# A fused binary-convolution and attention kernel: weight chunks for two blocks at once, packing one block behind the signs, and the last image's tiles moved to other memory

## The chip, the cores and the metric

The kernel runs on one core of one Trainium2 chip. The metric is the time of one execution in device microseconds (us). A ratio is the mean time of one kernel's undisturbed runs over the mean time of the kernel before in the same rounds on the same chip, with a 95% interval; it is therefore not exactly the ratio of the medians that are quoted beside it.

## The reference

Sixteen images of 256 channels and 28 x 28 pixels go through four layers. The two layers with sign weights, and the normalization between them, are where the change works:

```python
def layer0(x, weights, gamma, beta):              # first layer
    out = sign(x)                                  # forward value of the straight-through form
    scaling = mean(abs(weights), axis=(1, 2, 3))   # one number per output channel
    y = conv3x3(out, sign(weights)) * scaling      # (summed in slices of 64, saturating)
    yn = batchnorm(y) * gamma + beta
    return yn + x
# second layer: residual = prelu(x); clipped 3x3 convolution, fixed normalization, prelu, gate 1,
#               residual; then a 1x1 convolution, normalization, prelu, gate 2, residual.
#               gate = sigmoid(relu(mean(mix) @ w1 + b1) @ w2 + b2)
# third layer:  batchnorm -> sign -> conv3x3(sf * sign(w1)) -> prelu -> batchnorm -> sign
#               -> conv3x3(sf * sign(w2)) -> prelu -> batchnorm -> + x -> prelu
# fourth layer: attention over the pixels with 64 channels, projection, + x
```

## The kernel before

A 3x3 convolution of an image half ("block", 392 pixels) with sign weights is done in two ways. For five of six weight chunks the signs of two groups of 128 output channels are packed into one number, so 15 matmuls do the work of 30; the sixth chunk is done plainly with six matmuls, and two more unpack. `packed` is followed by a rounding on ScalarE and VectorE.

```python
def sign(k, g):                                     # one weight chunk of 384 KB, already loaded in st
    ...
    sg = tmp.tile([P, 3, 256], BF16, tag="sg", bufs=1)
    A.activation(sg, st, AF.Sign)                   # ScalarE
    V.scalar_tensor_tensor(dst[0][:, n], sg[:, :, P:], PACK, sg[:, :, 0:P], mult, add)   # VectorE: wpk
def add_up(k, g):                                   # sums of |w| for the scaling
    V.tensor_reduce(ab, st..., add, apply_absolute_value=True)                           # VectorE: ab
    return lambda: total_up(k, g, ab)               # TensorE "sumabs<-ones,ab", then VectorE "sf"
def both(first, second):                            # a step: sign + pack + reduce; its sum one block later
    return [Step(f.load, lambda: (f.work(), s.work())[1]) ...]

def packed(j):                                      # 15 matmuls of block j
    for n in range(5):
        for t in range(3): product(j, ..., w[0][:, n, t, :], ...)
    A.activation(r, pss[j], Identity, bias=rounding, scale=1/PACK); V.tensor_scalar(bs[j], r, -ROUND, None, add)

# sign_layer, for each block j:  packed(j); plain(j-1); post(j-1); signs of the next image;
#                                late();  late = steps.pop(0)()
```

The start loads the small parameters `vec`, the first image whole, and each weight chunk, which is signed and packed at once with the single `sg` buffer. At the end of the second layer two squeeze gates are computed, each by four small matmuls `hid` and four small matmuls `gate`. TensorE is given filler matmuls (`keep_busy(n)`, all on a tile `idle`) in front of and behind them, so that its clock stays up:

```python
keep_busy(14); g = gates(hidden_b(B, hidden_a(B)));  keep_busy(14)     # gate 1 of the last image
... conv1x1(b) ...
unit_u(b, 0); unit_u(b, 1, True)                    # u of the last image, tiles of tag "yu" in pool ph1
keep_busy(14); h = hidden_a(B + 1); ... g = gates(h)[:, 1] ...; keep_busy(14)          # gate 2
sg1, bg1 = norm("l2a", moments1, ...);  branch2(b, k, g) for both k    # gate updates that read u
# ph1 is released here; the third layer's padded image buffer "fpads" lies in the released memory
fpads = float_pads(ph, "fpads")                     # four clearings of its rim, on GpSimd
keep_busy(12)
```

## Time and profile before

| | us |
|---|---|
| median of 3 runs | 1153.67 (1153.47 to 1154.21) |
| span of the profiled run | 1151.9, mean granted clock 0.991 |
| TensorE busy | 1113.7 (97%) |
| first 30 packed matmuls loaded, by the weight loads | 19.74 |
| first gate ("hid") at the end of the second layer | 524.66 |
| second gate to the third layer's first convolution matmul | 539.10 to 547.30 = 8.20 |
| those first 30 matmuls | 7.65 |

The lines behind these numbers stand in the prediction below. In a timeline a row is start, duration, engine, kernel line, operation, output<-inputs, count, and in brackets the idle time before it with what ended it. A row with "x26" is 26 instructions run together. The rows "PE ... unused<-idle" are the fillers: the work is thrown away, but their spacing shows the clock, about 0.22 us at full clock ("warm" below) and 0.43 at half ("cold").

### The profile page before, as it was taken

The page shows a single profiled execution, that of the slowest core. Times are in us where ns is not written, and L with a number is a line of the kernel's source. Part 1 is how long each engine was busy: PE and PEld are TensorE (multiplying, and loading weights), DVE is VectorE, ACT ScalarE, POOL GpSimd, SP SyncE. Part 2 cuts the span into 40 slices and gives each one's busy share as a digit, 9 for nine tenths or more (in the row PEclk, how much of TensorE's full clock was granted, in tenths as well). Part 3 has the DMA queues.
Part 4 walks back from the last instruction along what each step waited for, and adds up shares of the span by engine and source line. Part 5 has one row for each costly group of instructions (what it writes and reads, how often), then busy time and mean ns, then how long its engine had stood idle before and what let it go on. Part 6 is the DMA issues. An engine that isn't in the chain of part 4 may idle for free.

```text
span 1151.9 us, 15800 instructions
## 1 busy us (share of the span) xinstructions
PE 1113.7 (97%) x6062; PEld 948.5 (82%) x6067; DVE 801.2 (70%) x1430; ACT 711.5 (62%) x1051; POOL 135.8 (12%) x134
## 2 busy tenths in 40 slices
PE   6998999999999999998999999999999999999995
PEld 6998989999999999994999998999955555555542
DVE  3775359899999999967576665566574667666565
ACT  4654445677777777765555554555576766767742
POOL 2000000000000000000000000000013443443421
PEclk9999999999999999999999999999999999999998
DMA  7553341222222231010680000000014355464422
GB/s 301 187 178 140 126 143 40 71 98 85 91 106 84 74 124 70 29 53 34 249 317 5 1 1 1 1 1 1 1 57 112 95 158 147 106 168 122 131 84 87
DMA packets 25973, 111.63 MB, mean 97 GB/s; under 512 B 3554, under 2 KB 6308, under 8 KB 25892
## 3 DMA queue, kind: packets, MB, share of 16 engines
q1 hardware_dynamic: 20436, 80.85, 20.0%
q0 software_dynamic: 5456, 29.71, 8.8%
q8 instruction: 50, 0.82, 0.3%
q14 instruction: 31, 0.25, 0.1%
HBM read 65.59 MB, written 44.96 MB: 96 GB/s over the span
## 4 chain that ended last, share of the span: by engine, by line
PE 79%; issue 5%; DVE 4%; ACT 2%; POOL 0%; POOLq 0%; ACTq 0%; DVEq 0%
PE cv L248 24%; PE cv L574 23%; PE sc L1127 7%; PE av L1148 7%; PE mi L1112 4%; PE sm L1188 4%; PE cv L678 3%; PE cv L267 2%; PE mi L1198 2%; PE unused L342 1%; PE sm L1148 1%; ACT fpads L933 1%; DVE r L1173 0%; PE hid L506 0%; PE gate L649 0%
## 5 line engine op out<-in xcount | busy, mean ns | idle before, releaser
L248 PE MATMUL cv<-fpads,wpk 128*128 128x392 f32 x1440 | 297.9, 360 | 11.3 <-DVE wpk L208 8.9
L574 PE MATMUL cv<-vs,w 128*128 128x392 f32 x1536 | 301.4, 354 | 0.0
L574 PEld LDWEIGHTS cv<-vs,w 128*128 128x128 f32 x1536 | 287.4, 190 | 1.6 <-issue 0.3
L248 PEld LDWEIGHTS cv<-fpads,wpk 128*128 128x128 f32 x1440 | 274.8, 194 | 15.7 <-issue 8.5
L963 DVE SCALAR_TENSOR_TENSOR p<-r,r,cv 128x392 f32<-128x392 f32 x128 | 78.6, 614 | 79.5 <-ACT r L960 79.5
L1131 ACT ACTIVATE es<-sc 112x784 f32<-112x784 f32 x112 | 87.2, 822 | 73.8 <-PE sc L1127 73.6
L248 PE MATMUL cv<-fpads,wpl 128*128 128x392 f32 x576 | 124.8, 352 | 0.0
L259 ACT ACTIVATE t<-cv,rounding 128x392 f32<-128x392 f32 x96 | 56.2, 586 | 88.0 <-PE cv L248 85.7
L248 PEld LDWEIGHTS cv<-fpads,wpl 128*128 128x128 f32 x576 | 108.9, 190 | 0.6
L1127 PE MATMUL sc<-q,k 64*112 64x392 f32 x448 | 89.0, 510 | 2.6 <-DVE k L1119 1.6
L960 ACT ACTIVATE r<-cv 128x784 f32<-128x784 f32 (+1 forms) x66 | 52.9, 805 | 60.0 <-PE cv L267 59.5
L260 DVE TENSOR_SCALAR uv<-t 128x392 fp32r<-128x392 f32 x96 | 35.0, 364 | 68.1 <-ACT t L259 68.1
L1148 PE MATMUL av<-es,va 112*64 112x392 f32 x448 | 80.8, 499 | 0.0
L1127 PEld LDWEIGHTS sc<-q,k 64*112 64x112 f32 x448 | 35.8, 172 | 43.3 <-issue 18.3
L1141 POOL TENSOR_TENSOR sum<-sum,es 112x784 f32<-112x784 f32 x32 | 68.5, 2139 | 2.5
L1148 PEld LDWEIGHTS av<-es,va 112*64 112x64 f32 x448 | 29.6, 136 | 47.4 <-issue 44.6
L103 DVE TENSOR_TENSOR vs<-pad 128x840 fp32r<-128x840 bf16 (+1 forms) x66 | 64.5, 1002 | 0.1
L481 ACT CAST n<-cv 128x784 int16<-128x784 f32 x32 | 26.0, 812 | 58.8 <-DVE l_parts L480 16.4
L1119 DVE COPY k<-mi 64x784 f32<-64x784 f32 x16 | 15.6, 976 | 64.2 <-ACT q L1118 64.2
L716 POOL DMA_DIRECT2D x2d<-x x16 | 8.5, 533 | 366.8 <-DVE x L710 304.0
L1202 DVE TENSOR_TENSOR p<-mi,p 128x784 f32<-128x784 f32 x30 | 29.2, 975 | 31.5 <-PE mi L1198 31.1
L1188 PEld LDWEIGHTS sm<-wv,p 128*112 128x112 f32 x448 | 46.7, 178 | 5.0 <-issue 2.6
(248 smaller groups left out, 1702.7 us busy)
## 6 DMA issues: line engine op xcount, KB each, us to landing
xs<-in_x_dram SPq DMA_DIRECT2D x32, 784.0 KB, 4.4
x2d<-x POOLq DMA_DIRECT2D x16, 784.0 KB, 3.6
xd<-p SPq DMA_DIRECT2D x16, 784.0 KB, 3.3
out_dram<-p SPq DMA_DIRECT2D x15, 784.0 KB, 5.3
p<-x2d SPq DMA_DIRECT2D x13, 784.0 KB, 9.0
p<-x2d POOLq DMA_DIRECT2D x13, 784.0 KB, 9.1
n0d<-n POOLq DMA_DIRECT2D x16, 392.0 KB, 2.7
n<-n0d SPq DMA_DIRECT2D x16, 392.0 KB, 3.1
```

The lines of the kernel that those rows point to most:

```text
L103: V.tensor_tensor(o, a, b, op)
L248: T.matmul(pss[j][:, mo, :HN].rearrange("p (a b) -> p a b", b=S), lhsT=lhsT, rhs=pads[:, j // 2 % 2, k, r:r + HR, c:c + S], start=start, s ...
L259: A.activation(r, pss[j][:, 0, :HN], AF.Identity, bias=rounding, scale=1.0 / PACK)
L574: T.matmul(ps.rearrange("p (a b) -> p a b", b=S), lhsT=w[:, k, c, u, mo * P:(mo + 1) * P], rhs=vs[:, b % 2, u, k, :, c:c + S], start=(n == 0),
L960: A.activation(r[:, mo], ps[:, mo, :HN], AF.Relu, scale=-1.0)
L963: V.scalar_tensor_tensor(p, r[:, mo], beta[:, mo:mo + 1], ps[:, mo, :HN], ALU.mult, ALU.add)
L1112: T.matmul(ps[:, h, :HN], lhsT=wqk[:, k, :], rhs=x[b][:, k, h * HN:(h + 1) * HN], start=(k == 0), stop=(k == 1),)
L1127: T.matmul(ps[:MC, h, :HN], lhsT=k_[rows, c * MC:(c + 1) * MC], rhs=qs[b][rows], start=True, stop=True)
L1131: A.activation(e, ps[:MC, :, :HN], AF.Exp, scale=0.125)
L1141: (V if late else nc.gpsimd).tensor_tensor(sums[b, late], sums[b, late], e, ALU.add)
L1148: T.matmul(ps[64 * h:64 * h + 64, :HN], lhsT=w, rhs=e[:, h, :], start=start, stop=stop)
L1188: T.matmul(ps[:MC, c * 64:(c + 1) * 64], lhsT=x[b][:, k, c * MC:(c + 1) * MC], rhs=wv[:, k, :], start=(k == 0), stop=(k == 1),)
```

## The change

Three things are intended: TensorE starts sooner, because two blocks use each weight chunk as it comes and the transfers are in the order of need; VectorE reduces before it packs, so the weight sums no longer wait; and the third layer's buffer can be cleared early, because the last image's `u` no longer lies in the memory that it takes. The core of the diff:

```diff
-    nc.sync.dma_start(out=vec, in_=d["vecs"])
+    nc.gpsimd.dma_start(out=vec, in_=d["vecs"])
@@ sign: returns the packing instead of doing it; two sg buffers at the start
-            sg = tmp.tile([P, 3, 256], BF16, tag="sg", name="sg", bufs=1)
-            A.activation(sg, st, AF.Sign, saturate=False)
-            V.scalar_tensor_tensor(dst[0][:, n], sg[:, :, P:], PACK, sg[:, :, 0:P], ALU.mult, ALU.add)
+            t = tmp.tile([P, 3, 256], BF16, tag=sg[0], name="sg", bufs=sg[1])
+            A.activation(t, st, AF.Sign, saturate=False)
+            return lambda: V.scalar_tensor_tensor(
+                dst[0][:, n], t[:, :, P:], PACK, t[:, :, 0:P], ALU.mult, ALU.add
+            )
@@ both: packing and sum run one block later
-        return [Step(f.load, lambda f=f, s=s: (f.work(), s.work())[1]) for f, s in zip(first, second)]
+        def work(f, s):
+            rest = f.work(), s.work()
+            return lambda: [r() for r in rest]
+        return [Step(f.load, lambda f=f, s=s: work(f, s)) for f, s in zip(first, second)]
@@ packed: blocks 0 and 1 take each chunk in turn
-        def packed(j):
+        def packed(*js):
             ...
             for n in range(5):
-                for t in range(3):
-                    product(j, ...)
+                for j in js:
+                    for t in range(3):
+                        product(j, ...)
@@ start: order of the transfers
-            load_x(0)
+            top, bottom = ((0, HR + 1),), ((HR + 1, S),)
+            load_x(0, rows=top)
+            signs[0].load()
+            load_x(0, rows=bottom)
+            for step in signs[1:]:
+                step.load()
+            load_x(1, rows=top + bottom)
+            load_x(2)
@@ end of the second layer
-                unit_u(b, 0)
-                unit_u(b, 1, True)
+                last = wpool.tile([P, 2, N], F32, tag="wa", name="last")
+                px = hidden_x(B + 1)
+                unit_u(b, 0, last[:, 0, :])
+                unit_u(b, 1, last[:, 1, :], True)
```

Cut: the first image's signs by half in the same way, one multiplication of `hidden_a` moved ahead (`hidden_x`), and the last two PSUM reads split by half. The number and order of fillers is not changed: 14, 14, 14, then 14 + 12.

More of the change, by code (lines that the diff above doesn't have):

```diff
@@ L188, in load_ahead, with sign_weights @@
         return [lambda s=s, t=t: (s.work(), t.load() if t else None)[0] for s, t in zip(steps, steps[n:] + [None] * n)]
-    def sign_weights(pool, dst, src, total, acc, stage=("st", 2), tmp=None, ab_tag="rn"):
+    def sign_weights(pool, dst, src, total, acc, stage=("st", 2), tmp=None, ab_tag="rn", sg=("sg", 1)):
         sts = {}
@@ L204, in sign @@
                 A.activation(dst[1], st, AF.Sign, saturate=False)
-                return
-            sg = tmp.tile([P, 3, 256], BF16, tag="sg", name="sg", bufs=1)
-            A.activation(sg, st, AF.Sign, saturate=False)
-            V.scalar_tensor_tensor(dst[0][:, n], sg[:, :, P:], PACK, sg[:, :, 0:P], ALU.mult, ALU.add)
+                return lambda: None
+            t = tmp.tile([P, 3, 256], BF16, tag=sg[0], name="sg", bufs=sg[1])
[3 more added lines that the diff above has]
+            )
         def add_up(k, g):
@@ L235, in split2, with sign_layer @@
         tt(dsts[1], st, dsts[0].bitcast(F32), ALU.subtract)
-    def sign_layer(pads, w, temp, sign, post, steps, moments, first=None):
+    def sign_layer(pads, w, temp, sign, post, steps, moments, first=None, together=1):
         pss = [None] * 2 * B
@@ L251, in product @@
             )
-        def packed(j):
-            pss[j] = conv_ps()
+        def packed(*js):
+            for j in js:
+                pss[j] = conv_ps()
             for n in range(5):
-                for t in range(3):
-                    product(j, 0, w[0][:, n, t, :], n, t, n + t == 0, n + t == 6)
-            r, bs[j] = temp("t1"), temp("uv", FR)
-            A.activation(r, pss[j][:, 0, :HN], AF.Identity, bias=rounding, scale=1.0 / PACK)
-            V.tensor_scalar(bs[j], r, -ROUND, None, ALU.add)
+                for j in js:
+                    for t in range(3):
+                        product(j, 0, w[0][:, n, t, :], n, t, n + t == 0, n + t == 6)
+            for j in js:
+                r, bs[j] = temp("t1"), temp("uv", FR)
+                A.activation(r, pss[j][:, 0, :HN], AF.Identity, bias=rounding, scale=1.0 / PACK)
+                V.tensor_scalar(bs[j], r, -ROUND, None, ALU.add)
         def plain(j):
@@ L271, in sign_image @@
         def sign_image(i):
-            for r0, r1 in ((0, HR + 1), (HR + 1, S)) if i == 0 else ((0, S),):
+            for r0, r1 in ((0, HR + 1), (HR + 1, S)) if i < together else ((0, S),):
                 sign(i, slice(r0, r1), lambda k: inner(pads[:, i % 2], k, r0, r1))
@@ L282, in sign_layer @@
                         first()
-                if j < 2 * B:
+                if j == 0:
+                    packed(*range(together))
+                elif together <= j < 2 * B:
                     packed(j)
@@ L348, in conv_seq_kernel, with load_x @@
             xs, ns = [None] * B, [None] * B
-            def load_x(b, integers=False):
-                xs[b] = ph.tile([P, 2, N], F32, tag="xs", name=f"xs{b}", bufs=4)
-                nc.sync.dma_start(out=xs[b], in_=d["x"][b])
+            def load_x(b, integers=False, rows=((0, S),)):
+                if not xs[b]:
+                    xs[b] = ph.tile([P, 2, N], F32, tag="xs", name=f"xs{b}", bufs=4)
+                for r0, r1 in rows:
+                    n = slice(r0 * S, r1 * S)
+                    nc.sync.dma_start(out=xs[b][:, :, n], in_=d["x"][b][:, :, n])
                 if integers:
@@ L364, in temp @@
                 return ph.tile([P, HN], dt, tag=tag, name=tag, bufs=2)
-            signs, sums_ = sign_weights(ph, w0, d["w0"], sf0, pss, ("yu", 6))
-            load_x(0)
-            A.activation(small.tile([P, 1], F32, tag="mv", name="root"), ones, AF.Sqrt)
-            for i, step in enumerate(signs):
-                step.load()
-                step.work()
-                if i in (2, 5):
-                    load_x(1 + i // 3)
+            signs, sums_ = sign_weights(ph, w0, d["w0"], sf0, pss, ("yu", 6), sg=("t1", 2))
+            top, bottom = ((0, HR + 1),), ((HR + 1, S),)
[6 more added lines that the diff above has]
+            load_x(2)
+            A.activation(small.tile([P, 1], F32, tag="mv", name="root"), ones, AF.Sqrt)
+            for step in signs:
+                step.work()()
             eye = ph.tile([P, P], F32, tag="rn", name="eye", bufs=4)
@@ L485, in conv_seq_kernel @@
             mom = halves_moments("l0")
-            sign_layer(fpads, w0, temp, sign0, post0, steps, mom)
-            load_x(0, True)
-            load_x(1, True)
+            sign_layer(fpads, w0, temp, sign0, post0, steps, mom, together=2)
+            for b in range(2):
+                xs[b] = None
+                load_x(b, True)
             keep_busy(30)
@@ L528, in full, with relu_neg @@
                 return ph.tile([P, N], F32, tag=tag, name=name, bufs=bufs)
-            def relu_neg(ap, bias=0.0, scale=-1.0):
+            def relu_neg(ap, bias=0.0, scale=-1.0, apart=False):
                 r = full("rn", "rn", 4)
-                A.activation(r if len(ap.shape) == 2 else halves(r), ap, AF.Relu, bias=bias, scale=scale)
+                for i in range(2) if apart else (slice(0, 2),):
+                    A.activation(
+                        r if len(ap.shape) == 2 else halves(r)[:, i], ap if len(ap.shape) == 2 else ap[:, i], AF.Relu,
+                        bias=bias, scale=scale,
+                    )
                 return r
@@ L627, in prelu_b, with hidden_x, hidden_a @@
                 )
-            def hidden_a(t):
-                x, y = sums_of(t)
-                p, r = (small.tile([P, 2, 2], F32, tag=f"g{i}", name=f"g{i}") for i in range(2))
-                tt(p, x, mix_x, ALU.mult)
-                tt(r, y, mix_y, ALU.mult)
+            def hidden_x(t):
+                p = small.tile([P, 2, 2], F32, tag="g0", name="g0")
+                return tt(p, sums_of(t)[0], mix_x, ALU.mult)
+            def hidden_a(t, p):
+                r = small.tile([P, 2, 2], F32, tag="g1", name="g1")
+                tt(r, sums_of(t)[1], mix_y, ALU.mult)
                 return hidden_sums(tt(p, p, r, ALU.add))
@@ L685, in conv1x1, with unit_u @@
                     us[b, mo] = ps
-            def unit_u(b, mo, vector=False):
+            def unit_u(b, mo, u=None, vector=False):
                 m, ps = slice(mo, mo + 1), us[b, mo][:, :, :HN]
-                u = full("yu", f"u{b}_{mo}", 6)
+                if u is None:
+                    u = full("yu", f"u{b}_{mo}", 6)
                 if vector:
-                    V.tensor_scalar(halves(u), ps, s3[:, m], c3[:, m], ALU.mult, ALU.add)
+                    for h in range(2):
+                        V.tensor_scalar(halves(u)[:, h], ps[:, h], s3[:, m], c3[:, m], ALU.mult, ALU.add)
                 else:
@@ L694, in unit_u, with unit_r @@
                 us[b, mo] = (u, ps)
-            def unit_r(b, mo):
+            def unit_r(b, mo, apart=False):
                 m = slice(mo, mo + 1)
                 u, ps = us[b, mo]
-                us[b, mo] = (u, relu_neg(ps, nc3[:, m], ns3[:, m]))
+                us[b, mo] = (u, relu_neg(ps, nc3[:, m], ns3[:, m], apart))
             def unit_b(b, mo):
@@ L735, in iteration @@
                 if b + 2 < B:
+                    xs[b + 2] = None
                     load_x(b + 2, True)
@@ L758, in iteration @@
                 conv_pair(b, 0, 0, 0)
-                h = hidden_a(b) if one else None
+                h = hidden_a(b, hidden_x(b)) if one else None
                 if ahead:
@@ L815, in iteration @@
                         conv_pair(b, 1, i, u)
+                    px = hidden_x(B)
                     rows_out(b, 1)
@@ L818, in iteration @@
                     prelu_b(b, 1)
+                    return px
             sc0 = bi0 = zb1 = nbi0 = None
@@ L842, in conv_seq_kernel @@
                 for b in range(B):
-                    iteration(b)
+                    px = iteration(b)
                 b = B - 1
                 keep_busy(14)
-                g = gates(hidden_b(B, hidden_a(B)))
+                g = gates(hidden_b(B, hidden_a(B, px)))
                 keep_busy(14)
@@ L865, in conv_seq_kernel @@
                 products(x2[b][:, 1, :], shift[:, 1:2], x2[b][:, 1, :], sum_vv[:, 1:2])
-                unit_u(b, 0)
-                unit_u(b, 1, True)
+                last = wpool.tile([P, 2, N], F32, tag="wa", name="last")
+                px = hidden_x(B + 1)
+                unit_u(b, 0, last[:, 0, :])
+                unit_u(b, 1, last[:, 1, :], True)
                 for k in range(2):
-                    unit_r(b, k)
+                    unit_r(b, k, k == 1)
                     unit_b(b, k)
                 keep_busy(14)
-                h = hidden_a(B + 1)
+                h = hidden_a(B + 1, px)
                 for k in range(2):
@@ L975, in conv_seq_kernel @@
             sign_layer(
-                fpads, w2a, temp, sign2a, post2(order, r1, mom), steps, mom, rest[0].work
+                fpads, w2a, temp, sign2a, post2(order, r1, mom), steps, mom, lambda: rest[0].work()()
             )
```

## The prediction

> **What bounds the kernel now.** I read four views in this order: the busy shares, TensorE's waits, the timelines around the longest of those waits, and the windows with the granted clock. The first two:
>
> ```profile
> PE 1113.7 (97%) x6062; PEld 948.5 (82%) x6067; DVE 801.2 (70%) x1430; ACT 711.5 (62%) x1051; POOL 135.8 (12%) x134
> PE cv L248 <- DVE wpk L208: 8.9, 2, 8.6
> PE sumabs L219 <- DVE ab L213: 6.1, 6, 2.5
> PE cv L248 <- POOL fpads L90: 2.0, 1, 2.0
> ```
>
> TensorE is busy 97% of 1151.9 us, so about 38 us of idle time is all that reordering can touch, plus stretches where it is busy but slow. The wait rows (us in total, times, longest) name three places, and the change aims at each: the start, where the first weights arrive late; the small weight-sum matmuls waiting for a VectorE reduction; and the border between the second and third layers, where the padded image buffer is cleared late. VectorE's 70% and ScalarE's 62% matter only where a matmul waits for them.
>
> The start (start us, duration, engine, line, operation):
>
> ```profile
> 5.70 1.39 ACT L359 ACTIVATE fpads<-xs 128x420 fp32r<-128x420 f32 x3 [3.46 <-DMA xs<-in_x_dram]
> 7.00 0.82 ACT L207 ACTIVATE sg<-st 128x768 bf16<-128x768 f32 x1
> 7.86 0.56 DVE L208 SCALAR_TENSOR_TENSOR wpk<-sg 128x384 fp32r<-128x384 bf16 x1 [3.80 <-ACT sg L207]
> 8.45 0.84 ACT L207 ACTIVATE sg<-st 128x768 bf16<-128x768 f32 x1 [0.23 <-DVE wpk L208]
> 13.91 0.56 DVE L208 SCALAR_TENSOR_TENSOR wpk<-sg 128x384 fp32r<-128x384 bf16 x1 [0.91 <-ACT sg L207]
> 14.53 5.21 PEld L248 LDWEIGHTS cv<-fpads,wpk 128*128 128x128 f32 x18 [0.65 <-DVE wpk L208]
> ```
>
> The five weight chunks are signed (0.84) and packed (0.56) strictly in turn, because there is a single sg buffer: 1.46 us a chunk, while one block has only three matmuls for it. The last 18 (three of block 0, all of block 1) start at 14.53 and are done at 19.74.
>
> The end of the first layer:
>
> ```profile
> 103.64 0.14 DVE L223 SCALAR_TENSOR_TENSOR sf<-sumabs,sf 128x2 f32<-128x2 f32 x1
> 106.03 0.83 ACT L207 ACTIVATE sg<-st 128x768 bf16<-128x768 f32 x1
> 106.89 0.56 DVE L208 SCALAR_TENSOR_TENSOR wpk<-sg 128x384 fp32r<-128x384 bf16 x1 [3.11 <-ACT sg L207]
> 107.37 1.03 DVE L213 TENSOR_REDUCE ab<-st 128x256 f32<-128x768 f32 x1
> 108.54 0.58 PE L219 MATMUL sumabs<-ones,ab 128*128 128x1 f32 x4 [1.12 <-DVE ab L213]
> ```
>
> VectorE idles 3.11 us for the sign, with the reduction, which doesn't need it, queued behind the packing. TensorE then waits 1.12 us for the reduction.
>
> The border:
>
> ```profile
> 539.57 5.77 PE L342 MATMUL unused<-idle 128*128 128x512 bf16 x26
> 543.83 1.03 DVE L710 SCALAR_TENSOR_TENSOR x<-u,gates,x 128x784 f32<-128x784 f32 x1
> 545.98 2.53 ACT L933 ACTIVATE fpads<-x,l2a_c,l2a_r 128x420 fp32r<-128x420 f32 x4 [3.32 <-DVE x L710]
> 546.12 0.53 POOL L716 DMA_DIRECT2D x2d<-x  x1 [13.78 <-DVE x L710]
> 547.30 7.65 PE L248 MATMUL cv<-fpads,wpk 128*128 128x392 f32 x30 [1.96 <-POOL fpads L90]
> 549.00:551.00 2.00, 2.00 (x8) 2.00 (x8) 0.00 (x0) 0.84 (x1) 0.00 (x0) 0.50 1.04 436
> ```
>
> The signs wait for both gate updates of the last image (to 545.74), the clearing for the store queued before it, and the convolution starts at 547.30, 1.96 us after the filler matmuls end (539.57 + 5.77 = 545.34). The last row is a window of 2 us; its third value from the right is the granted clock, 0.50, seen from 548 to about 551.3. So idling there is paid twice.
>
> **What the Trainium skill says.** "TensorE: Matmul & The Clock Gate", Part 1, says that the array runs at half clock until a free-running window of about 3.4 us was busy, and again after an idle one. The trace agrees: 0.50 for some 3.3 us after the border. Its opening table calls ScalarE's and VectorE's queues strict FIFO; the 3.11 us row is that, a ready reduction stuck behind a packing. "DMA: Bandwidth & Descriptors", Specifications, puts the fabric ceiling at 435 GB/s; half-microsecond windows from 8.5 to 15 us show 353 to 458. The same table has GpSimd's DMA slower to its first byte (about 1 us against 0.6), which matters for the moved parameter load only; its first use in the new order is still far ahead of the first packing.
>
> **The change, part by part.** The instruction order of the built program has the same matmuls on TensorE, so only waits and clock can change.
>
> Matmul spacing first. Warm, 15 take 3.00 us: 0.20 each. At the border 30 weight loads take 547.29 to 554.60, 7.31 instead of 6.0, so 1.3 us is lost in about 3.4 us at half clock: 0.20 x 3.4/2.1 = 0.33 cold. At the start, 18 in 5.21 us means (5.21 - 3.6)/0.13 = 12 cold ones: TensorE turns warm only near 18.6 (the clock column reads 1.00 there, but the spacing says otherwise).
>
> (A) The start. Landing before: the first image (784 KB, issued 1.20) 5.70, the fourth weight chunk 11.5; both fit 2.75 + bytes/403 KB per us + 0.85. Now the queue starts 0.46 us earlier with half an image; in the new order the estimate is: top half 4.2, chunk 0 5.2, bottom half 6.1, chunks 1 to 5 at 7.1, 8.1, 9.0, 10.0, 11.0, second image 13.0. ScalarE: top half to 5.3, sign 0 to 6.1, bottom half to 7.1, then a sign as each chunk lands. Packings end at about 6.7, 8.5, 9.5, 10.5 and 11.5: two sg buffers uncouple the two engines. TensorE starts at 6.8 with six matmuls a chunk, 2.0 us cold, so it is never starved; it warms after a whole busy window, between 10.2 and 13.6, say 11.7. By then 15 are done; 15 x 0.20 ends at 14.7. The first 30 took until 19.74: 5.0 us saved (4.3 to 5.6 for the two ends). The next eight matmuls then hide the rounding of block 0; the second image (four pieces from 15.6 on ScalarE) is just in time at 16.2.
>
> (B) First layer, packing one behind. The five steps on the third layer's weights have three waits: 2.45 (at 96.15), 1.12 and 1.12, 4.69 us. In the new order VectorE runs previous packing, previous sum, reduction, so the reduction ends near 105.4 instead of 108.4, and the matmul could use it from 107.4: the wait goes. Its chunk was loaded at 85 and is no obstacle. After the 2.45 wait, 15 matmuls took 4.12 us of loads instead of 2.82: another 1.3. Sum 6.0.
>
> (C) The border. The last image's u now lies outside the released memory, so the clearing waits for the last square (540.86 + 0.19), and the signs for the normalization's coefficients (543.91), no more for 545.74. Splitting the last PSUM reads by half and taking one multiplication early gives about 0.4 us (0.2 from the second relu beginning on one half, 0.2 from the earlier start and the multiplication). Signs begin at 543.6, the first is ready at 544.2; but the 26 fillers run to 545.34 - 0.4 = 544.95 and now come last. Start 544.95 instead of 547.30: 2.35. Without the gap no half clock: 1.3. Sum 3.7.
>
> (D) Third layer, the same packing: waits of 0.71, 0.37 and 0.36; VectorE lost 0.2 in the later ones to the sign and a whole packing (0.56) before the first reduction. About 1.1.
>
> Everything else is bound by TensorE at the same spacing. 5.0 + 6.0 + 3.7 + 1.1 = 15.8; 1153.67 - 15.8 = 1137.9. I take half a microsecond off for clock windows that fall badly: 1138.4.
>
> **Rivals.** (1) The gain at the start is the loads' to give: if half-image loads move slower or the chunk is late, TensorE waits for DMA instead of packing. Against it, chunk 4 has some 2 us of slack in my table; a rate of 350 instead of 403 would cost about 1 us: 1139.4. (2) The fillers at the border come out cold: windows are free-running, and all of this stage moves by 11 us. At half clock some eight fewer of them fit into 3.4 us and the convolution starts 1.7 us later; for it speaks the half clock seen at 528 after similar gaps. Time 1140. (3) The change merely moves VectorE's work: packing in the next step could delay the rounding or the statistics, and the three PSUM buffers fill. Against it, 70% load and 3.11 us of idle time in just these steps. If B gave only half, 1141.5. (4) Nothing is gained at the start because ScalarE, which has to sign the second image after both roundings, holds block 2: costs up to 1 us. (5) More than summed: other half-clock stretches (at 528, where TensorE also idles first) vanish: 1136.
>
> **Range and chances.** The rivals cost 1 to 3.5 us and seldom come together; two at once give 1143, all in my favour 1135. Range 1134.5 to 1143. Two per cent is 23 us, down to 1130.6, which needs half as much again as everything I find idle or slow here: 3%. Slower by 2% would need a new stall of 23 us plus the gains: 1%.
>
> **What would show it.** A: first convolution matmul near 6.8, and the first three-matmul plain group at 14 to 15.5 instead of 19.74. B: no wait of the sums for ab at the first layer's end, no half clock after it. C: fillers followed by the convolution without a gap, no 0.50 behind it. D: sums' total wait under 1 us. I'd be wrong if TensorE's waits name DMA at the start, if fillers are spaced 0.4 us, or if matmuls wait for uv in the steps.

## More of the kernel before

One more stretch of the kernel before, its timeline of TensorE behind the first gate's small matmuls:

```profile
526.35 4.87 PE L342 MATMUL unused<-idle 128*128 128x512 bf16 x14
530.75 3.31 PE L678 MATMUL cv<-z,fw 128*128 128x392 f32 x16
```

The 14 fillers took 4.87 us, where the same 14 ahead of the second gate took 3.19: part of them ran at half clock.

## The result, and the profile after

The changed kernel took 1141.88 us (median of 4 runs, 1137.91 to 1144.1), the kernel before 1153.57 in the same rounds (4 runs, 1152.39 to 1154.21). The ratio is 0.9896 (0.9866 to 0.9926): 1.0% less time, within the 2% that counts as the same. The prediction was 1138.4 in a range of 1134.5 to 1143.0. Notable is the spread: 6 us, where the kernel before has 1.8.

The profiled run has a span of 1138.8 us, 13.1 less than before. Following the same instruction in both traces divides this:

| from the start to | before | after | gained up to here | by this part | predicted |
|---|---|---|---|---|---|
| packed matmuls of block 2 | 21.41 | 17.39 | 4.0 | A: 4.0 | 5.0 |
| first gate ("hid") | 524.66 | 513.78 | 10.9 | B: 6.9 | 6.0 |
| 30 packed weights of the third layer loaded | 554.60 | 542.38 | 12.2 | C: 1.3 | 3.7 |
| end | 1151.9 | 1138.8 | 13.1 | D: 0.9 | 1.1 |

**The waits.** In the list of TensorE's waits (total, times, longest) the rows "sumabs" and "POOL fpads" are gone, 6.1 and 2.0 us before. The first packing, which everything waits for, still leads the list (8.9 before). Next comes a wait in the last layer, `sc` for `o`, 4.4 us against 4.5, which the change doesn't touch and the prediction didn't list. The wait ahead of the two gates is longer than the 1.8 us before:

```profile
PE cv L254 <- DVE wpk L208: 7.9, 1, 7.9
PE hid L526 <- DVE g L103: 2.3, 2, 1.3
```

**The start**, from the timeline of all engines (the last two rows from TensorE's weight loads):

```profile
6.50 1.21 DVE L208 SCALAR_TENSOR_TENSOR wpk<-sg 128x384 fp32r<-128x384 bf16 x1
7.62 0.91 ACT L373 ACTIVATE fpads<-xs 128x364 fp32r<-128x364 f32 x2 [1.16 <-DMA xs<-in_x_dram]
9.44 0.56 DVE L208 SCALAR_TENSOR_TENSOR wpk<-sg 128x384 fp32r<-128x384 bf16 x1 [1.73 <-ACT sg L207]
12.43 0.56 DVE L208 SCALAR_TENSOR_TENSOR wpk<-sg 128x384 fp32r<-128x384 bf16 x1 [0.42 <-ACT sg L207]
10.05 5.24 PEld L254 LDWEIGHTS cv<-fpads,wpk 128*128 128x128 f32 x24 [0.39 <-DVE wpk L208]
15.80 1.05 PEld L254 LDWEIGHTS cv<-fpads,wpl 128*128 128x128 f32 x6 [0.51 <-ACT t L268]
```

The lower half of the first image could be signed only at 7.62 (the prediction had it landed at 6.1), and ScalarE, which works in order, signs chunk 1 behind it. So chunk 1 is packed at 10.00, not 8.5, and the fifth at 12.99, not 11.5. The first packing took 1.21 us instead of 0.56. The 30 matmuls are loaded at 15.29. The last row is a wait that the prediction didn't draw: the plain matmuls behind the 30 stand 0.51 us for ScalarE's rounding of the packed ones. In the kernel before, the same loads follow at 19.74 without a gap, since block 1's packed matmuls lay between.

**The end of the first layer**: the reduction now directly follows the packing and sum of the step before, and the weight sums start at 99.11 without waiting.

```profile
95.78 0.54 DVE L208 SCALAR_TENSOR_TENSOR wpk<-sg 128x384 fp32r<-128x384 bf16 x1
96.31 1.04 DVE L215 TENSOR_REDUCE ab<-st 128x256 f32<-128x768 f32 x1
99.11 0.50 PE L221 MATMUL sumabs<-ones,ab 128*128 128x1 f32 x4
```

**The border** to the third layer:

```profile
526.45 0.58 PE L526 MATMUL hid<-g,se 128*128 128x2 f32 x4 [1.25 <-DVE g L103]
527.63 1.01 PE L675 MATMUL gate<-hidden,se 128*128 128x2 f32 x4 [0.61 <-ACT hidden L667]
528.51 8.55 PE L353 MATMUL unused<-idle 128*128 128x512 bf16 x26
532.79 2.53 ACT L967 ACTIVATE fpads<-x,l2a_c,l2a_r 128x420 fp32r<-128x420 f32 x4 [1.41 <-DMA st<-in_w2a_dram]
536.71 6.02 PE L254 MATMUL cv<-fpads,wpk 128*128 128x392 f32 x30
```

The signs are early, as intended: four pieces from 532.79, so the first is there at about 533.4. (The row puts their wait down to a DMA; the coefficient `l2a_c`, which they need too, is finished on VectorE at 532.63, and the idle time is the same 1.41 us in the traces of runs 3, 5, 9 and 11, so the wait is more likely for that.) But the 26 fillers, which took 5.77 us before, took 8.55, and the convolution stood behind them until 536.71. From gate to convolution it is now 9.08 us, 0.88 more than before. The windows (start:end, length, TensorE busy and count, granted clock, DMA share, GB/s) say why:

```profile
526.00:528.00 2.00, 0.94 (x6) 0.84 0.02 4
530.00:532.00 2.00, 2.00 (x6) 0.50 0.55 141
534.00:536.00 2.00, 2.00 (x10) 0.96 1.01 420
```

TensorE was given half clock from 527.3 to 534.2. The prediction's second rival, cold fillers, had happened, and worse than it was drawn.

### The profile page after: what moved, and what is told of

Its sections match the earlier page's. It is cut to its first block, busy times and chain, and to the rows that moved or that the text cites. A ratio compares the mean times of both kernels' runs of the same rounds, so it can differ in the third digit from the quotient of the medians. Undisturbed runs are those within 1.5% of the kernel's fastest.

```text
span 1138.8 us, 15813 instructions
## 1 busy us (share of the span) xinstructions
PE 1109.4 (97%) x6067; PEld 944.5 (83%) x6067; DVE 802.2 (70%) x1431; ACT 711.5 (62%) x1054; POOL 136.2 (12%) x135
## 4 chain that ended last, share of the span: by engine, by line
PE 93%; DVE 4%; ACT 2%; issue 0%; DMA 0%; ACTq 0%; DVEq 0%; POOLq 0%
PE cv L254 33%; PE cv L598 25%; PE sc L1161 7%; PE av L1182 7%; PE mi L1146 4%; PE cv L704 4%; PE sm L1222 4%; PE cv L276 3%; PE unused L353 2%; PE mi L1232 2%; PE sm L1182 1%; PE sumabs L221 1%; PE hid L526 1%; PE gate L675 1%; DVE r L1207 0%
## 5 line engine op out<-in xcount | busy, mean ns | idle before, releaser
L254 PE MATMUL cv<-fpads,wpk 128*128 128x392 f32 x1440 | 291.7, 355 | 8.0 <-DVE wpk L208 7.9
L254 PEld LDWEIGHTS cv<-fpads,wpk 128*128 128x128 f32 x1440 | 270.7, 191 | 10.2 <-POOL worst L1043 7.9
```

Source lines behind the costliest of these rows:

```text
L254: T.matmul(pss[j][:, mo, :HN].rearrange("p (a b) -> p a b", b=S), lhsT=lhsT, rhs=pads[:, j // 2 % 2, k, r:r + HR, c:c + S], start=start, s ...
```

## The experiments

My theory after this: (T1) the fillers at half clock, a consequence of TensorE idling ahead of the gates' small matmuls, ate most of the border's gain and, by the chance of when they occur, make the spread; (T2) the start is short of its prediction because of when the transfers land and because TensorE is cold; (T3) the packing one block behind is worth what was predicted and needs nothing else. Each kernel ran in five rounds beside the kernel before, four kernels to a chip.

### 1. Clearing four buffers later

```diff
-            for p in pads:
-                nc.gpsimd.memset(p, 0.0)
-            for t in (w_1, w_2):
-                nc.gpsimd.memset(t, 0.0)
+                if j in (1, 3, 5, 7):                      # in post0, that is inside the first layer
+                    V.memset((*pads, w_1, w_2)[j // 2], 0.0)
```

> The changed kernel with the clearing of the second layer's two padded buffers and of the two squeeze weights moved off GpSimd, from the start to VectorE inside the first layer. Held-packing theory (the five tiny VectorE operations and the first packing, 1.21 us instead of 0.56, are held until GpSimd's run of clearings ends at 7.65): the tiny operations end before 6.0, the first packing ends at 7.1 or before, the first convolution matmul starts at 7.3 or before instead of 7.88, and[...] the fourth group of 15 comes up to 0.6 us earlier; time 0.3 to 0.6 us less than the changed kernel. Load theory (the lower half of the first image lands only at 7.6, and ScalarE's queue behind it sets chunk 1): the tiny operations may end earlier, but chunk 1 is packed at 10.0 as before, and the end of the first 30 matmuls (15.3 by the weight loads) moves by less than 0.3 us; time within 0.3 us.

Measured: 1141.9 us (4 runs), ratio 0.9904 (0.9890 to 0.9918). The local half of the held-packing theory is right: five tiny VectorE operations that took up to 2.92 us took 0.17 each, and the packing behind them 0.56.

```profile
5.05 0.17 DVE L148 TENSOR_SCALAR l_half<-vec 128x2 f32<-128x2 f32 x1 [5.05 <-DMA vec<-in_vecs_dram]
6.85 0.56 DVE L208 SCALAR_TENSOR_TENSOR wpk<-sg 128x384 fp32r<-128x384 bf16 x1 [1.35 <-ACT sg L207]
10.35 6.34 PEld L254 LDWEIGHTS cv<-fpads,wpk 128*128 128x128 f32 x24 [1.02 <-DVE wpk L208]
```

But nothing comes of it: the first matmul comes at 7.56 (I had expected 7.3 or before), chunk 1 is packed at 10.30 in this run, and the 24 matmuls behind it end at 16.69, later than in the first trace, because TensorE turned warm only at 14.82 (11.93 in the first trace, by the clock records in the traces). That its wait of 1.02 us for chunk 1 is the reason is not shown: run 4 waited 0.28 us there and turned warm at 13.06, run 10 waited 0.46 and turned warm at 11.74. The load theory stands, with the clock as its companion.

### 2. More fillers ahead of the second gate

```diff
-                keep_busy(14)
+                keep_busy(20)
                 h = hidden_a(B + 1, px)
```

> The changed kernel with 20 instead of 14 filler matmuls ahead of the last hidden-layer matmuls of the gate (TensorE idles 1.25 us there in the profiled run). Theory of the cold fillers: the two windows at half clock behind the gate come from this idle time; without it the 26 fillers before the third layer take about 5.8 us instead of 8.55, the convolution follows the gate by about 6.4 us instead of 9.08, and the time falls by 2 to 2.7 us against the changed kernel, with a smaller spread. Rival: the half clock comes from the gate's own gaps (0.69 us and tiny matmuls), or from the phase of the clock's window alone: fillers stay at 0.33 us on average in most runs, time within 0.7 us of the changed kernel, or worse by the 0.1 us of extra fillers.

Measured: 1140.93 us (4 runs, 1139.0 to 1143.65), ratio 0.9892 (0.9878 to 0.9907). TensorE's timeline in the profiled run, which was the slowest of the four:

```profile
517.20 6.05 PE L353 MATMUL unused<-idle 128*128 128x512 bf16 x14
531.59 0.61 PE L675 MATMUL gate<-hidden,se 128*128 128x2 f32 x4 [0.61 <-ACT hidden L667]
532.06 5.77 PE L353 MATMUL unused<-idle 128*128 128x512 bf16 x25
```

The second gate did what the theory says: its fillers at full clock, the convolution 5.91 us behind it (537.50) instead of 9.08. But in this run the fillers behind the *first* gate, which has the same idle time ahead of it, were cold: 6.05 us instead of the 3.18 of the changed kernel's trace. What one gate gained the other lost, so the expected 2 us are not there. This showed that one has to look at both.

### 3. Fewer fillers behind the second gate

```diff
             rest[0].load()
-            keep_busy(12)
```

> The changed kernel without the 12 filler matmuls at the head of the third layer (14 left behind the gate instead of 26). If the fillers set the start of the third layer's convolution, and not the signs, which are ready 4.8 us after the gate began: with cold fillers at 0.43 us the 14 end about 6 us after the gate's end and the convolution starts 2.0 to 2.8 us earlier than now; time 2 to 2.7 us less. If they come out warm in a run (0.22 us), TensorE idles about 1.7 us and the convolution starts at half clock: gain about 1.5 us. Rival: the signs or the clearing set the start: no gain.

Measured: 1138.93 us (5 runs, 1138.15 to 1143.18), ratio 0.9887 (0.9871 to 0.9903). The median falls by 2 to 3 us as expected, the ratio by less, with two long runs among the five. The trace is of one of these, with both gates cold, the first throughout (6.07 us for its 14 fillers) and the second in part:

```profile
531.35 0.61 PE L675 MATMUL gate<-hidden,se 128*128 128x2 f32 x4 [0.61 <-ACT hidden L667]
531.81 4.87 PE L353 MATMUL unused<-idle 128*128 128x512 bf16 x14
```

Fourteen fillers end before the signs are there, and the convolution follows the gate by 5.90 us. So it was the fillers, not the signs or the clearing, that set the start.

### 4. The last image's u back in the released memory

```diff
-                last = wpool.tile([P, 2, N], F32, tag="wa", name="last")
-                unit_u(b, 0, last[:, 0, :]); unit_u(b, 1, last[:, 1, :], True)
+                unit_u(b, 0); unit_u(b, 1, None, True)
```

> The changed kernel with the last image's u tiles back in the memory that is released (so the clearing of the padded buffers waits for both gate updates and is queued behind the store, as before the change). With the fillers at half clock until 8.1 us behind the gate this is hidden: signs about 2 us later than 533.35, at about 535.3, still before the fillers end at 536.7; time within 0.5 us of the changed kernel. If the fillers are warm in most runs: 1.5 to 2.3 us slower. If the move itself was what the border gained, 2.4 us slower.

Measured: 1142.19 us (6 runs, 1140.5 to 1145.25), ratio 0.9917 (0.9904 to 0.9931). Within half a microsecond was too narrow: the means say 1.3 to 1.6 us more than the changed kernel's, the ratio 0.0021 to 0.0025, that is 2.4 to 2.9 us; the intervals overlap. The trace has the convolution 8.19 us behind the gate (528.08 to 536.27), 0.27 of it a wait for the clearing. The changed kernel has 9.08 in one trace and, as run 12 shows, 7.56 in another; only against the first is the move worth nothing.

### 5. Both gates filled

```diff
-                keep_busy(14)
+                keep_busy(19)
                 g = gates(hidden_b(B, hidden_a(B, px)))
 ...
-                keep_busy(14)
+                keep_busy(20)
                 h = hidden_a(B + 1, px)
 ...
             rest[0].load()
-            keep_busy(12)
+            keep_busy(10)
```

> The changed kernel with 19 fillers ahead of the last-but-one and 20 ahead of the last gate's hidden matmuls instead of 14 each, and 24 instead of 26 behind the last gate. Theory: the half-clock stretches at the two gates are windows in which TensorE idled about 1.1 us ahead of hid and 0.6 us ahead of gate; the earlier run with 20 kept the last gate warm (26 fillers in 5.8 us) but its middle gate ran at half clock (14 fillers in 6.05 us instead of 3.18). With both filled: 14 fillers behind the middle gate in about 3.2 us, 24 behind the last in about 5.3 us, no clock below 0.95 between 500 and 540 us, the distance from the middle hid to the third layer's convolution 20.3 us or less (22.9 in the changed kernel, 22.4 in each of the two runs with one of the gates cold); time 1136 to 1139 with little spread. Rival: the idle time ahead of hid is not what cools it (gate gaps or free phase are): one of the two stretches is at half clock again, distance 22 or more.

Measured: 1138.09 us (4 runs, 1137.6 to 1138.68), ratio 0.9871 (0.9857 to 0.9885). Everything in the expectation came out:

```profile
516.35 3.18 PE L353 MATMUL unused<-idle 128*128 128x512 bf16 x14
528.52 0.61 PE L675 MATMUL gate<-hidden,se 128*128 128x2 f32 x4 [0.61 <-ACT hidden L667]
528.99 5.34 PE L353 MATMUL unused<-idle 128*128 128x512 bf16 x24
534.41 5.96 PE L254 MATMUL cv<-fpads,wpk 128*128 128x392 f32 x30
```

From the first gate's hid (514.67) to the convolution it is 19.74 us, no window of 2 us has a reduced granted clock up to 1120 us, and the spread is 1.1 us. The prediction's own arithmetic for the border (8.20 - 2.35 = 5.85 us from gate to convolution) is met at 5.89. It has the lowest median and beats both kernels.

### 6. Fillers at the start

```diff
+            if together == 2:
+                keep_busy(9)                       # ahead of the first block
 ...
+                if n == 0 and len(js) == 2:
+                    keep_busy(4)                   # between chunk 0 and chunk 1
```

> The changed kernel with nine fillers on TensorE ahead of the first convolution matmul (from the clearing of their operand at about 3.6 us on) and four between the first and the second weight chunk. Theory of the cold start: the loads by which the first 30 matmuls end (15.3 in the profiled run of the changed kernel, 15.7 to 16.7 in four others) are late because TensorE is at half clock until a window is busy throughout; with it warm, the end is set by the fifth packing (12.99) plus six warm matmuls: 14.3 to 14.6 in each run, and the fourth group of 15 begins 0.7 to 1.9 us earlier; time 1 to 1.5 us less than the changed kernel on average. Rival, loads only: TensorE is starved by the chunks anyway and the end stays at 15.3 or later, or the second image's signs (ScalarE) hold block 2: time within 0.5 us.

Measured: 1140.63 us (4 runs, 1139.22 to 1141.57), ratio 0.9890 (0.9876 to 0.9905). Locally it worked, nearly as far as expected:

```profile
10.32 4.48 PEld L254 LDWEIGHTS cv<-fpads,wpk 128*128 128x128 f32 x24 [0.61 <-DVE wpk L208]
```

The loads end at 14.80 (15.29 to 16.69 without), 0.2 later than expected because the fifth packing was 0.25 later. The first gate came at 513.27, against 513.78 and 514.76 in the changed kernel's two traces. In the time this is not to be told from the gates' chances: in this run both gates were partly cold (14 fillers 4.87, 26 fillers 7.46 us).

### 7. Packing in turn again

```diff
-            return lambda: V.scalar_tensor_tensor(
-                dst[0][:, n], t[:, :, P:], PACK, t[:, :, 0:P], ALU.mult, ALU.add
-            )
+            V.scalar_tensor_tensor(dst[0][:, n], t[:, :, P:], PACK, t[:, :, 0:P], ALU.mult, ALU.add)
+            return lambda: None
```

> The changed kernel with each chunk packed in the step that signs it, as before the change, all else left in. If packing one block behind is what took the waits of the weight sums away: the wait of the sums for the reduction is back (6 to 9 us in all over the first and third layers), the first layer ends 6 to 7 us later, the third another 1; time 7 to 8 us more than the changed kernel, near 1149. Rival (the first layer gains from the shifted start and the loads, not from the packing): 3 us more or less.

Measured: 1149.8 us (6 runs, 1146.69 to 1152.78), ratio 0.9969 (0.9953 to 0.9986). That is 7.9 us (medians) to 8.9 us (ratios, 0.0077 of 1152.5, against run 12) more than the changed kernel. The row of the waits is back, with the kernel before's six waits and 6.1 us:

```profile
PE sumabs L220 <- DVE ab L214: 6.1, 6, 2.4
```

The rival's 3 us are out. The first gate is at 523.16, 8.4 us later than in run 12. Part of it is again the clock: in this trace it was reduced from 92 to 100 us, behind the first of these waits, as it had been for one window before the change.

### 8. The packing one block behind as the only change

The diff of `sign` and `both` above, applied to the kernel before with its single `sg` buffer.

> The kernel before with the packing one block behind the signs as its only change. If the parts of the change add: 7 to 8 us less than before, near 1145.5 (ratio 0.9935), the sums' wait for the reduction gone from TensorE's waits, the start (fourth group of 15 at 21.4 us) and the border (convolution 8.2 us behind the gate) as before. If the parts depend on each other (for instance the packing needs two sg buffers, since with one the next sign waits for the packing): 3 to 5 us less.

Measured: 1145.1 us (5 runs, 1143.82 to 1145.85), ratio 0.9932 (0.9919 to 0.9944), so 7.0 us (medians) to 7.8 us (ratio) less than before. The parts add up: no sums' wait in the list, the start nearly as before (block 2's 15 loads at 20.70, against 21.24) and the border too (gate to convolution 8.20 us).

### 9. Fillers at the gates and at the start

Runs 5 and 6 in one kernel.

> The changed kernel with both sets of fillers: those at the two gates (19, 20, and 24 behind) and those at the start (nine ahead, four between the first chunks). If the two gains are independent: the first 30 matmuls end near 14.8 by the loads, the distance from the middle hid to the third layer's convolution is near 19.7 us, no half clock from 500 to 540 us; time 1.3 to 1.9 us less than with the gate fillers alone, near 1136.5, which beats both kernels. Rival (time gained at the start is lost to a later wait, since ScalarE's and the loads' pace set the first blocks): within 0.6 us of the gate fillers alone, 1138.

Measured: 1138.9 us (4 runs, 1138.37 to 1139.61), ratio 0.9876 (0.9861 to 0.9891): no gain over run 5 (0.8 us more by the medians, 0.6 by the ratios, where the rival allowed 0.6); the rival is right, and the trace shows its reason. In this run the lower image half could be signed only at 9.15, 1.1 to 1.65 us later than in the ten other traces of this start, though the instructions of the transfers are the same:

```profile
9.15 0.91 ACT L377 ACTIVATE fpads<-xs 128x364 fp32r<-128x364 f32 x2 [2.63 <-DMA xs<-in_x_dram]
```

Chunk 1, signed behind it, was packed 1.3 us later than in run 6, TensorE starved and went back to half clock from 10.1 to 13.6 us. The gates were both warm, with 5.89 us from gate to convolution. Whether fillers at the start are worth anything on average stays open: one profiled run gained by them and one did not.

### 10. Warm gates, u inside the released memory

Runs 5 and 4 in one kernel.

> The changed kernel with warm gates (fillers 19, 20 and 24) and the last image's u tiles back in the released memory. With warm fillers nothing hides the later clearing any more: the signs wait for both gate updates and for the clearing behind the store, about 1.9 us later than with the tiles outside (532.6 to 534.5, counted from a gate at 528.5), and TensorE idles about 1.5 us ahead of the convolution and may cool: 1.5 to 3 us more than with the gate fillers alone, near 1140. Rival (the move is worth nothing in any state): within 0.5 us, 1138.

Measured: 1143.23 us (5 runs, 1140.88 to 1144.84), ratio 0.9913 (0.9898 to 0.9929): 5.1 us (medians) or 4.8 us (ratios) more than run 5, beyond the 3 that I had allowed.

```profile
528.10 5.12 PE L353 MATMUL unused<-idle 128*128 128x512 bf16 x23
535.82 5.37 PE L254 MATMUL cv<-fpads,wpk 128*128 128x392 f32 x18 [2.60 <-POOL fpads L90]
```

The gate is at 527.63, so the convolution is 8.19 us behind it: 2.30 later than with `u` outside, all of it open to view as 2.60 us of idle time. That cooled TensorE, and the 30 matmuls took 7.65 us instead of 5.96. The third piece, 1.0 us, is a half-clock stretch at the attention's entry near 845, where TensorE idles 1.55 us for a VectorE copy in each trace whose waits I read; it shows up in some runs and not in others. 2.3 + 1.7 + 1.0 = 5.0. That the sum meets the 5.1 of the medians is chance: the two traces differ by only 4.1 us, because this one reached its first gate 0.88 us earlier. The part that belongs to `u` is the 4.0 of the border.

### 11. Warm gates, the old start

The start as it was (parameters first, whole images, one `sg` buffer, blocks one at a time), with the fillers of run 5.

> The changed kernel with warm gates (19, 20, 24) and the start put back as it was before the change: parameters loaded first, whole images, weight chunks signed and packed strictly in turn with one sg buffer, one block at a time. The start's share of the gain then comes out without the lottery at the gates: the fourth group of 15 begins at 21.0 to 21.6 us instead of 17.2 to 18.6, so 3 to 4 us more than with the gate fillers alone, near 1141.5. Rival (the prediction's 5.0): near 1143.

Measured: 1141.76 us (4 runs, 1140.86 to 1142.54), ratio 0.9899 (0.9884 to 0.9914): the start is worth 3.7 us (medians) or 3.2 us (ratios), not 5.0. Its 15 loads for block 2 began at 22.40, against 18.11 in run 5, so this trace shows 4.3. In it, too, a transfer came late: the wait for the fourth chunk was 1.73 us, where experiment 8 had 1.17.

### 12. The changed kernel once more

> The changed kernel itself once more, beside the others on one chip. Theory of the chance clock windows: its runs again spread over 3 us or more, at 1138 to 1144, the granted clock lower in the longer runs; the profiled run shows half clock behind at least one of the two gates and the sum of its fillers' times there accounts for its distance above the run with filled gates. Rival (the spread is the chip's or the loads'): the spread here is as small as that of the kernel with the filled gates, under 1.5 us.

Measured: 1141.0 us (4 runs, 1139.99 to 1142.33), ratio 0.9892 (0.9877 to 0.9908). The spread is 2.3 us, between my two numbers (3 or more, under 1.5), but with the first four runs it is 6.2 over eight, and run 5's is 1.1. The profiled run:

```profile
529.26 7.26 PE L353 MATMUL unused<-idle 128*128 128x512 bf16 x26
```

Only one half-clock window here (528.9 to 532.3), so from gate (528.61) to convolution (536.17) it is 7.56 us. Against run 5's trace its profiled run is 3.65 us longer (1142.33 to 1138.68). From first hid to convolution 1.67 of these are lost, at the attention's entry (half clock near 843) 1.0, and between 948 and 985 another 1.1, in the attention, 0.62 of it a wait for a VectorE copy at 976 that run 5's trace doesn't have. So my expectation, that the gates alone account for it, holds for not quite half of the difference in this pair.

### What the traces have in common

Gate-to-convolution times in all fourteen traces, in us:

| u of the last image | behind the second gate | traces | from gate to convolution |
|---|---|---|---|
| inside | warm or partly cold | before, runs 4, 8, 10 | 8.20, 8.19, 8.20, 8.19 |
| outside | two windows at half clock | first trace after, run 7 | 9.08, 9.05 |
| outside | one window | runs 1, 6, 12 | 7.56, 7.57, 7.56 |
| outside | warm, or 14 fillers | runs 2, 5, 9, 11; run 3 | 5.91, 5.89, 5.89, 5.89; 5.90 |

The clearing makes a floor at 8.2, the signs one at 5.9, and the fillers' clock decides how much of the difference is had.

The half-clock stretches can be counted too. Behind the second gate there was one in eight of the nine traces with 14 fillers ahead of it, and in none of the five with 20. Behind the first gate there was one in six of the ten traces with 14 fillers, and in none of the four with 19. This is the best evidence that the idle time ahead of the gates' matmuls lets the clock fall; that it did not fall each time is the chance in it.

## Why the prediction was right, and which term was mis-sized

The time, 1141.88, lies in the predicted range of 1134.5 to 1143.0, and "same" was the likely class. The mechanism of all four parts is confirmed, A's as a whole only: its edits (parameters on GpSimd's queue, image halves, order of the loads, two sg buffers, two blocks to a chunk) were taken out together in run 11, so which of them earns the time is not shown. Nor have the split PSUM reads and the early multiplication a run of their own. The total saved is 12 us by the ratio (0.0104 of 1153.6), 13.1 between the profiled runs, where 15.8 were summed and 15.3 predicted.

- **A, the start (5.0 predicted).** 4.0 between the first traces, 3.2 to 3.7 by run 11 against run 5. The step that failed is the table of landings: "bottom half 6.1" was 7.62 and in one run 9.15, and since ScalarE has it ahead of chunk 1, "Packings end at about 6.7, 8.5, 9.5, 10.5 and 11.5" became 7.71, 10.00, 11.04, 12.01 and 12.99. This is rival 1, "half-image loads move slower", at 1139.4. The clock estimate, 11.7, held in the first trace (11.93) and in run 10, but in the seven other traces without fillers at the start TensorE turned warm at 13.06 to 14.82. Half a microsecond more is the wait for the rounding: "The next eight matmuls then hide the rounding of block 0" failed, since these eight wait for it. The parameters' first use was not "far ahead of the first packing" in effect: the small operations on them came at 4.76 (3.5 us after the issue on GpSimd's queue, where Sync's took 1.9 before, but with other loads under way), were held until about 7.7 and the first packing with them, 0.65 us. (The 458 GB/s of one half-microsecond window lies above the ceiling of 435 that the prediction quotes; the mean from 8.5 to 15 us is 410, below it.) The tell-tale "first convolution matmul near 6.8" came at 7.88, and the first plain group at 15.80 missed "14 to 15.5".
- **B, packing one behind (6.0).** 6.9 between the traces. With D, 7.0 to 7.8 alone (run 8) and 7.9 to 8.9 when taken out (run 7), where the prediction has 7.1. The step was right, its waits and the order on VectorE as drawn; rival 3 (work merely moved) is refuted by the list of waits. It is somewhat under-sized, since a wait costs more than its row shows: from the unpacking to the next block's first matmul, each step with a wait of 1.12 us took 2.08 (106.90 to 108.98), and without it 0.72 (103.55 to 104.27), which makes 1.36. In run 7 a second half-clock window comes on top.
- **C, the border (3.7).** 1.3, of which 0.6 was gained at the first gate, by luck of the clock (13.25 us from the first hid to the second before, 12.67 after), and only 0.7 at the border. The step: "the 26 fillers run to 545.34 - 0.4 = 544.95 and now come last". That they come last was right; that they would still take 5.77 us was not. They took 8.55 and, in run 12, 7.26. Rival 2 named this and put the convolution 1.7 us late; against run 5 it was 1.7 us late with one cold window and 3.2 with two. Runs 2, 3 and 5 show it by taking the cause away: the convolution then follows at 5.9 us, for which the prediction's working gives 5.85. The other half of the term, no half clock behind the border, held: 30 matmuls in 6.02 instead of 7.65 us.
- **D, third layer (1.1).** 0.9 between the traces, with no sums' wait left. Right.
- **The half microsecond for clock windows "that fall badly"** was too small. Run 5 is about 3 us shorter than the changed kernel (medians 1138.09 against 1141.88 and 1141.0; by the ratios 2.4 to 2.9, the intervals overlapping); how much of this is the gates is known for one pair of traces, 1.67 of 3.65 (run 12). That run 5 lands on the predicted 1138.4 is partly luck, errors that cancel: in its trace A gained 3.1 of the predicted 5.0, but B 6.9 of 6.0 and C 4.6 of 3.7.
- **Rival 5** (other half-clock stretches vanish, 1136) happened at the first gate in the profiled run, 3.18 us for its fillers instead of 4.87; it is a throw of the dice from run to run, as run 2's 6.05 shows. **Rival 4** (ScalarE holds block 2) did not show: block 2 begins right behind the unpacking in every trace; what ScalarE held was the plain group ahead of it, by 0.5 us.

What stays open is whether the spread of the changed kernel comes from the gates alone. Filling them took it from 6.2 us over eight runs to 1.1 over four, but the attention's entry and the landing of the start's loads vary too, and four runs are few. The other two kernels with both gates filled and `u` outside spread by 1.2 (run 9) and 1.7 us (run 11).

## What to carry to other kernels

Filler matmuls that keep the clock up are work in the queue: if they run at half clock they become the thing that is waited for, so size them by the end of what they cover, and see that TensorE doesn't idle in front of them. Shortening a chain in one place moves everything behind it relative to the clock's windows; a stretch that was warm by luck before is not warm by construction, and the spread of the runs can tell of it sooner than the median. When a load order is changed by estimate, give each landing its own error and follow the one that another engine's in-order queue hangs on.

## What the Trainium skill lacked or had wrong

- "TensorE: Matmul & The Clock Gate", Part 1, gives an idle window of about 3.4 us as what brings the half clock back. The length agrees: the half-clock stretches are 6.83 us (527.34 to 534.17, after) and 3.42 us (528.89 to 532.31, run 12), two windows and one. But no window was idle here. Laying the grid of 3.41 us back from these stretches, the window ahead was still 54% busy with matmuls in the first trace after (1.84 of 3.41 us), 53% ahead of the first gate in run 2, and 46% in run 12, and in the kernel before it was busy for 1.45 of 3.41 us ahead of the stretch at the border in which the prediction saw the page confirmed; windows with 69% and 71% (ahead of the first gate, run 12 and first trace) stayed warm. These shares are worked out from the timelines, not counted by the hardware. They are no rule either: a window with 1.86 of 3.41 us busy at the attention's entry, 55%, stayed warm in the first trace after (from 841.38) and was followed by half clock in run 12 (from 839.51). Under "A second HAM failure mode" the page does tell of half clock from frequent short idle times in another kernel; which partly busy windows cool, it doesn't say.
- "SBUF — State Buffer", Who interferes with whom, says that a VectorE operation in a two-port mode and a GpSimd operation exclude each other for a whole instruction. The traces agree with this, as far as they go: five TENSOR_SCALAR operations on two elements took up to 2.92 us while GpSimd cleared buffers, and 0.17 in run 1 without those clearings. What the page doesn't give is how long a row of GpSimd instructions can hold them: in the kernel before they were held 1.40 us, to 4.03, about the end of the first of two long clearings; in the first trace after until about 7.7, past the rest of one long clearing, a second and some ten short ones.
- No page tells how much a transfer's landing varies between runs of one program. Here the same half of an image, the third transfer in its queue, was signed as soon as it had landed, at 7.50 to 8.09 us in ten traces and at 9.15 in one.
